# Order of steps at the passage into layer 1 and in its loop, and the place of the last row tile's listing, in a four-layer graph network

## The chip, the cores and the metric

One Trainium2 chip, one core, one launch. The metric is device microseconds (us) of the whole launch. TensorE (PE) multiplies matrices, VectorE (DVE), ScalarE (ACT) and GpSimd (POOL) work element by element, and SyncE (SP) issues most of the transfers (DMAs). Each engine works through its own queue in order, and semaphores make one engine wait for another.

## The reference

The input is a matrix `x` of 2708 nodes by 128 features and a symmetric-patterned adjacency `adj` of 2708 by 2708, about 0.6% of it non-zero. Four layers follow each other, each `x = x + layer(relu(layernorm(x)), adj)`:

```
layer 0:  msg = adj.T @ h;  msg / adj.sum(axis=0)[:, None]
layer 1:  s = h @ msg_w[:, :D].T ; d = h @ msg_w[:, D:].T
          messages[i, j] = gelu(s[i] + d[j] + msg_b)
          agg[i] = sum_j adj[i, j] * messages[i, j]
          layernorm(gelu([h, agg] @ upd_w.T + upd_b) + h) * ln_w + ln_b
layer 2:  a GRU cell on relu((adj @ h) @ W_msg.T + b_msg)
layer 3:  two attention heads, masked by adj > 0 and the diagonal
```

The change lies in the end of layer 0 and in layer 1.

## The kernel before

**Layer 0.** Nodes are cut into 22 tiles of 128 rows (the last has 20), and these into 6 groups of four. `order` runs over columns of groups `c` and, in each, row groups `s`; a "cut" (c, s) is one 512x512 piece of `adj`. `work_cut` (from line 366) transposes the cut on PE into `p_T` (L403), has ACT copy it out and sum it (`aT`, L410), multiplies it on PE (`sums`, L388), and, between these, takes one step at a time from a generator: `next_steps(c, s)` gives, by stage, the finishing work of the column before (`lift`, `spread`, `sum_rows` L260, `sum_squares` L270, `normal_rows` L137, `last_destinations`). `list_cut` has DVE list each cut's non-zeros: for each row of a 128x128 block the eight largest values (MAX8, L356) and their columns (FIND_INDEX8, L358). The last column (c = LAST = 5, tiles named `z`) is worked among the cuts of column 4, and `list_last` lists some of its rows.

**What layer 1 prepares for a row tile t.** `count_some` or `count_rows` counts the non-zeros of each row and block (`rows_n`), `rank` turns counts into first slots by a matmul (`p_r`, L551, copied to `ends`), `spread_ends` and `select_rows` make a step function over 128 slots per block (`sel`, L558 and L601), which SP shifts by one row through a DMA (`later`, L620 and L621), and `finish_rows` subtracts (`sel - later`, L625), which leaves a one-hot row for each slot. The values are split in three bf16 parts (the "rests"): lead (`lead_of`, ACT L568), rest (DVE L571, in the passage `less_lead` L586), its cast on ACT (L572, in the passage L590) and the last part on POOL (L573, L591, with L580 and L581 behind). `fetch` (PE L639, read out on ACT as `lead`, L640) brings the values into the slots, `place` (DVE L652 to L673) picks the one of each slot and its column (`where`), `pass_on` (PE `p_w` L689, ACT `where_T` L691, SP L693) and `spread_columns` (SP L699) send the columns through DRAM to all partitions, and `columns` (DVE L973) makes them one-hot (`cols`). `put_values` (POOL L956) and `put_more` (ACT L965) make the weights. `destinations`, `take_lead` and `split_rest` (PE L232, ACT L240, DVE L247, ACT L253, POOL L254) make `d`, also in three parts, for a group of tiles; `sources` and `sources_rest` (PE L710, DVE L728, ACT L568, DVE L571, ACT L572, POOL L573) make `s`.

**The loop.** `period(t)` has six steps k. In each, `combine` (PE `p_m`, L1012 with `sel` and L1016 with `cols`), `activate` (ACT `g`, L1024, with two `p_m` buffers) and `gather` (PE `agg`, L1037) work on tile t; around them stand the columns and weights of t+1, the fetch and place of t+2, rank, selection, rests and finish of t+3 and the count of t+4. `update(g, step)` finishes a group of four tiles over eight later periods; steps 2, 3, 5 and 6 (and 0) have DVE work. `sources` runs in even periods. `list_late` lists, on DVE, blocks that layer 0 left out (rows 17 to 20 and, by `LAST_AT`, the ends of rows 6 to 16) from tiles `cols_a` that SP loads a period ahead (`load_late`); two blocks at k = 1, the rest at k = 5. The last row tile of 20 rows is listed in one go with its blocks side by side on the partitions (`load_wide`, `list_wide`), and `place_wide` copies the result to its place with twelve small DMAs: in period `WIDE_AT` = 17. The order in every queue is the order of the code (`manual_schedule`).

Before period 0, `run(...)` and `opening` hold what has no earlier period to stand in. In the text below a number in brackets is a tile or a group: `finish_rows(2)`, `split_rest(4)`.

Of the kernel before, what the change touches and what calls it, by code (L numbers as in the profile page):

```python
# [20 lines left out]
F32 = mybir.dt.float32  # L21
# [9 lines left out]
P = 128  # L31
N = 2708
# [28 lines left out]
def listed_layers(ctx: ExitStack, tc: tile.TileContext, x, adj, w, out, flag):  # L61
# [454 lines left out]
    def next_steps(c, s):  # L516

        off = 1 if c < LAST - 1 else 0
        stage = s - 1 - off
        if stage == -1:  # L520
            return lift(c - 1)
        if stage == 0:
            return spread(c - 1)
        if stage == 1:
            return sum_rows(c - 1)
        if stage == 2:
            return sum_squares(c - 1)
        if stage == 3:
            return normal_rows(h, c - 1)
        return last_destinations() if stage == 4 and c == LAST - 1 else ()  # L530

    def last_destinations():
        destinations(LAST - 2)
        yield
        pass_on(0)
        project(0)
        turn_sums(LAST)
        yield

    def list_last(n):  # L540
# [41 lines left out]

    def less_lead(t):
        dst, src = values_of(t)
        rest = state["x", t] = opener.tile([P, NB, S], F32, name="hot")
        nc.vector.tensor_tensor(rest, src, dst[0], ALU.subtract)  # L586

    def pass_rest(t):
# [144 lines left out]
    for i, (c, s) in enumerate(order):  # L733
        g0, gk = GROUPS[s]
        list_cut(c, s, g0)
        if i == 0:
            state["f", 0] = factors(*state.pop(("m", -1)))
            list_cut(c, s, g0 + 1)
            state["m", 1] = moments(tiles_of(xs, *GROUPS[1]), "n4")
            list_cut(c, s, g0 + 2)  # L740
            state["f", 1] = factors(*state.pop(("m", 1)))
            list_cut(c, s, g0 + 3)
        else:
            for n in range(g0 + 1, g0 + gk):
                if c > 0 and s == (2 if c < LAST - 1 else 1) and n == g0 + 1:
                    invert(c - 1)
                list_cut(c, s, n)
            if c == LAST - 1:
                for n in {0: range(FIRST), 1: range(FIRST, 4), 2: range(4, HELD), LAST: range(NT - 2, NT)}.get(s, ()):
                    list_last(n)  # L750
                if s == 0:
                    count_some(0, FIRST)
                if s == 1:
                    count_some(FIRST, 1)
        if i + 1 < len(order):
            mask_near(*order[i + 1])
        if i > BEHIND and i - 1 - BEHIND + RING < len(order):
            load_cut(*order[i - 1 - BEHIND + RING])
        for z in {(LAST - 2, 3): (0,), (LAST - 2, 4): (1,), (LAST - 2, 5): (2,), (LAST - 1, 0): (3,), (LAST - 1, 2): (4,), (LAST - 1, 3): (5,)}.get(
            (c, s), ()  # L760
        ):
            load_cut(LAST, z)
        if (c, s) == (LAST - 1, 2):
            shift_rows(0)
        if c > 0 and s == (2 if c < LAST - 1 else 1):
            turn_sums(c - 1)
        if (c, s) == (LAST - 1, LAST):
            turn_rows(LAST - 2)
        work_cut(c, s, first_steps(s) if c == 0 else next_steps(c, s))
        if c > 1 and s == 3:  # L770
            split_rest(c - 2)
        if (c, s) == (LAST - 1, 3):
            pass_rest(0)
        if c > 1 and s == 0:
            turn_rows(c - 2)
        if c > 1 and s == 1:
            destinations(c - 2)
        if c > 1 and s == 2:
            take_lead(c - 2)
        if c == LAST - 1:  # L780
            if s == 1:
                ranked = rank(0, FIRST, bank("p_r"))
            for z in PARTS.get(s, ()):
                mask_near(LAST, z)
                work_cut(LAST, z)
            if s == 1:
                nc.vector.tensor_copy(*ranked)
                spread_ends(0)
                select_rows(0)
                lead_of(*values_of(0))  # L790
            if s == 2:
                less_lead(0)
                finish_rows(0)
            if s == 3:
                for q in range(2):
                    fetch(0, q)
            if s == LAST - 1:
                place(0)
                lead_of(*values_of(2))
                less_lead(2)  # L800
                for _ in lift(LAST):
                    pass

        if (c, s) == (1, 2):
            nc.sync.dma_start(msg_wT, w["msg_wT"])
        if (c, s) == (2, 3):
            nc.sync.dma_start(msg_b, w["msg_b"].partition_broadcast(P))
            nc.gpsimd.tensor_copy(src_self[:, 0, :], msg_wT[:, 0, :])
            nc.gpsimd.tensor_tensor(src_self[:, 1, :], msg_wT[:, 0, :], msg_wT[:, 1, :], ALU.add)

    write_one()

    pass_rest(2)
    lead_of(*values_of(1))
    take_lead(LAST - 2, pool.tile([P, 4, D], F32, bufs=1, name="part_x"))
    add(LAST)
# [12 lines left out]

# [31 lines left out]
    with (  # L861
# [9 lines left out]
        def count_rows(t):  # L871
            some = work.tile([P, NB, S], BF16, name="some")
            nc.vector.tensor_scalar(some, val[:, t, :, :], 0.0, None, ALU.is_gt)
            with nc.allow_low_precision("counts up to 8"):
                nc.vector.reduce_sum(rows_n[:, t, :], some, AX.X)

        def load_late(t):

            units = late_blocks[(t - 1) * AT_ONCE : t * AT_ONCE] if t > 0 else []
            if not units:  # L880
                return
            wide = N - LAST * CH
            flat_cols = work.tile([P, AT_ONCE * JB + wide], F32, name="cols_a")
            cols = flat_cols[:, 0 : AT_ONCE * JB].rearrange("p (b e) -> p b e", e=JB)
# [23 lines left out]
        def list_late(t, first, last):  # L908
# [6 lines left out]
        WIDE_AT = (len(late_blocks) + AT_ONCE - 1) // AT_ONCE + 1  # L915
        pieces = [(b, min(WIDE, NB - 1 - b)) for b in range(0, NB - 1, WIDE)]

        def load_wide():
            cols = work.tile([P, AT_ONCE * JB + N - LAST * CH], F32, name="cols_a")
            cols = state["wide"] = cols[:, 0 : AT_ONCE * JB].rearrange("p (b e) -> p b e", e=JB)  # L920
            for i, (b, k) in enumerate(pieces):
                nc.sync.dma_start(
                    cols[i * TAIL : (i + 1) * TAIL, 0:k, :],
                    adj[FULL * P : N, b * JB : (b + k) * JB].rearrange("r (b e) -> r b e", e=JB),
                )

        def list_wide():
            cols = state.pop("wide")
# [198 lines left out]
        def period(t, opening):  # L1127
# [6 lines left out]
            for k in range(GB):  # L1134
# [3 lines left out]
                if k == 0 and c and begun:  # L1138
                    pass_on(t + 1)
                    spread_columns(t + 1)  # L1140
                if k == 1 and a:
                    nc.vector.tensor_copy(*rank(t + 3, 1, rpool.tile([P, CH], F32, tag="r", name="p_r")))
                    spread_ends(t + 3)
                if k == 1 and last:
# [18 lines left out]
                    lead_of(*values_of(t + 3))  # L1163
                if k == 1:
                    list_late(t, 0, EARLY)
                    if t == WIDE_AT:
                        list_wide()
# [25 lines left out]
                if k == 4 and a and not begun:  # L1193
                    select_rows(t + 3)
                    describe_rest(t + 3)
                if k == (4 if begun else GB - 1) and a:
                    finish_rows(t + 3)
                if k in (0, 3):
                    load_next()
                if k == 4:  # L1200
                    load_late(t + 1)
                    if t + 1 == WIDE_AT:
                        load_wide()
                for g, step in updates.pop((t, k), ()):
                    update(g, step)
                if k == GB - 1:
                    list_late(t, EARLY, None)
                    if now and NT - 2 <= t + 4 < NT:
                        count_rows(t + 4)


# [11 lines left out]
        def take_pair(g):  # L1223
# [6 lines left out]
        )  # L1230
        opening = {
            1: ((turn_rows, 4), (fetch_both, 1), (select_rows, 2), (put_more, 0, 1)),
            2: ((destinations, 4), (put_more, 0, 2), (put_more, 0, 3), (place, 1), (take_lead, 4), (finish_rows, 2)),
            3: ((split_rest, 4), (pass_on, 1), (spread_columns, 1), (put_more, 0, 4), (put_more, 0, 5)),
            4: ((fetch_both, 2), (find_rows, 1), (put_values, 1)),
            5: ((place, 2),),
        }
# [880 lines left out]
```

## Time and profile before

| what | value |
|---|---|
| time of the launch, median of 3 | 987.94 us (986.31 to 989.44) |
| profiled execution: its time, its span | 986.58 us, 984.8 us |
| busy share PE, DVE, ACT, POOL | 93%, 81%, 54%, 45% |
| mean granted TensorE clock | 0.968 |
| the loop of layer 1, first L1016 to last L1045 | 205.8 to 543.5 us |

Times within the launch are microseconds from the start of the span. A row of the timeline gives start, duration, engine, line, operation, output and input, the count, and in brackets how long the engine had been idle and who ended that. A row of waits gives who waited for whom, the total, the number of times and the longest. In a table of windows each engine has its busy time, and behind the engines stand the granted clock (1.00 is full speed), the share of the DMA engines and GB/s. A line number can be that of a helper, so the tile's name tells which step it is.

### The profile page before, as it was taken

How to read it: one execution, taken by the hardware profiler on the slowest of the kernel's cores; microseconds unless marked ns; L12 is line 12 of the kernel's file. 1: busy time of each engine (PE TensorE's matmuls, PEld its weight loads, DVE VectorE, ACT ScalarE, POOL GpSimd, SP SyncE). 2: the span in 40 equal slices, each digit the busy share in tenths (PEclk: the TensorE clock that was granted, in tenths of full speed). 3: DMA queues.
4: the chain of work that ended last, by engine and by line, in shares of the span. 5: the costliest groups of instructions: out<-in, count | busy, mean ns of one | idle time of the engine just before them, and what ended most of it. 6: DMA issues, size and time to landing. Idle time of an engine off the chain costs nothing. (4 is left out here: it accounts for less than half of the span.)

```text
span 984.8 us, 21973 instructions
## 1 busy us (share of the span) xinstructions
PE 911.1 (93%) x7948; PEld 742.5 (75%) x7948; DVE 797.0 (81%) x2753; ACT 531.8 (54%) x1561; POOL 444.1 (45%) x524
## 2 busy tenths in 40 slices
PE   6799999768999999899999999999789999999983
PEld 3465556558999999898999444444678999999972
DVE  7999999788988989889674756566689877997793
ACT  5766776656666756676566123433222553655242
POOL 5402221369976787969765634444111300430132
PEclk9999999978999999999999899999899999999996
DMA  9899998325543434323215355564301674456000
GB/s 334 286 354 365 359 368 296 125 94 160 169 129 117 149 115 135 120 81 132 91 62 190 119 190 208 194 237 134 93 6 57 211 245 151 145 186 208 1 17 15
DMA packets 81736, 163.61 MB, mean 166 GB/s; under 512 B 9100, under 2 KB 27056, under 8 KB 81618
## 3 DMA queue, kind: packets, MB, share of 16 engines
q1 hardware_dynamic: 62518, 129.98, 40.8%
q10 hardware_dynamic: 19100, 32.13, 9.0%
q8 instruction: 64, 1.05, 0.5%
q14 instruction: 54, 0.44, 0.1%
HBM read 115.47 MB, written 30.87 MB: 149 GB/s over the span
## 5 line engine op out<-in xcount | busy, mean ns | idle before, releaser
L1327 PE MATMUL att<-hv,wt 128*128 128x129 f32 x1672 | 195.7, 278 | 7.9 <-DVE wt L1297 6.4
L956 POOL TENSOR_SCALAR put<-count,line,value 128x128 f32<-128x128 f32 x176 | 197.6, 1134 | 11.1 <-DVE value L673 10.4
L1327 PEld LDWEIGHTS att<-hv,wt 128*128 128x128 f32 x1672 | 191.9, 194 | 10.9 <-DVE wt L1297 8.9
L1016 PE MATMUL p_m<-d,cols 128*128 128x128 bf16 (+1 forms) x1452 | 162.6, 221 | 9.2 <-DVE cols L973 4.3
L1012 PE MATMUL p_m<-s,sel 128*128 128x128 bf16 x1452 | 162.4, 221 | 5.0 <-ACT g L1024 4.9
L1297 DVE SCALAR_TENSOR_TENSOR wt<-row,lift,mask 128x1024 f32<-128x1024 f32 (+1 forms) x132 | 138.8, 1083 | 22.2 <-PE att L1327 22.2
L121 POOL TENSOR_TENSOR n_r<-n_r,minus_half 128x4 f32<-128x4 f32 (+1 forms) x28 | 38.9, 1389 | 237.7 <-DVE n_r L120 236.0
L1037 PE MATMUL agg<-put,g 128*128 128x128 f32 (+1 forms) x968 | 126.8, 284 | 0.0
L1037 PEld LDWEIGHTS agg<-put,g 128*128 128x128 f32 x968 | 116.2, 196 | 2.4 <-issue 0.2
L388 PE MATMUL sums<-a,h 128*128 128x512 f32 x220 | 113.9, 613 | 1.6 <-ACT h L137 1.6
L1488 PE MATMUL p_agg<-a,hs 128*128 128x512 f32 (+2 forms) x264 | 108.8, 554 | 2.8 <-DMA a<-adjT 2.8
L1012 PEld LDWEIGHTS <-sel 128*128 128x128 bf16 x1452 | 103.9, 99 | 9.0 <-issue 8.3
L1016 PEld LDWEIGHTS <-cols 128*128 128x128 bf16 (+1 forms) x1452 | 101.9, 99 | 10.1 <-DVE cols L973 5.0
L1024 ACT ACTIVATE g<-p_m 128x512 f32<-128x512 f32 x132 | 72.7, 552 | 63.8 <-PE agg L1037 45.0
L403 PEld LDWEIGHTS p_T<-ident,a 128*128 128x128 f32 (+1 forms) x440 | 55.4, 144 | 60.7 <-issue 43.1
L965 ACT ACTIVATE put<-mine,value 128x128 f32<-128x128 bf16 x308 | 100.6, 392 | 0.0
L358 DVE FIND_INDEX8 col<-val,a 128x8 uint16<-128x128 f32 x327 | 91.6, 298 | 0.0
L410 ACT ACTIVATE aT<-p_T 128x512 f32<-128x512 f32 (+2 forms) x132 | 71.1, 541 | 27.5 <-PE p_T L403 26.6
L1488 PEld LDWEIGHTS p_agg<-a,hs 128*128 128x128 f32 (+1 forms) x264 | 47.5, 193 | 50.6 <-issue 46.3
L403 PE MATMUL p_T<-ident,a 128*128 128x128 f32 (+1 forms) x440 | 70.5, 281 | 11.9 <-DMA a<-in_adj 6.2
L1450 ACT ACTIVATE hs<-hs 128x1354 f32<-128x1354 f32 (+1 forms) x44 | 58.5, 1330 | 39.9 <-DMA hs<-in_adj 39.5
L356 DVE MAX8 val<-a 128x8 f32<-128x128 f32 x327 | 79.4, 289 | 0.0
(297 smaller groups left out, 1529.0 us busy)
## 6 DMA issues: line engine op xcount, KB each, us to landing
hs<-in_adj SPq DMA_DIRECT2D x42, 677.0 KB
adjT<-aT ACTq DMA_DIRECT2D x50, 512.0 KB
a<-adjT SPq DMA_DIRECT2D x20, 1280.0 KB
a<-in_adj SPq DMA_DIRECT2D x24, 1024.0 KB
spread<-passed SPq DMA_DIRECT2D x22, 704.0 KB
later<-sel SPq DMA_DIRECT2D x22, 616.0 KB
cols_a<-in_adj SPq DMA_DIRECT2D x11, 320.0 KB
row<-own_d ACTq DMA_DIRECT2D x10, 256.0 KB
```

Of the source, the lines that this page charges most:

```text
L356: nc.vector.max(val[0:m, n, b, :], v)
L358: nc.vector.max_index(col[0:m, n, b, :], val[0:m, n, b, :], v)
L388: nc.tensor.matmul(accs[c][:, 0:w], h0[0:m, n, :], a[0:m, n - g0, t0 * P - lo : t0 * P - lo + w], start=(n == 0), stop=(n == NT - 1),)
L403: nc.tensor.transpose(p[0:k, i * iw + q * P : i * iw + q * P + m], a[0:m, q, e : e + k], ident[0:m, 0:m])
L956: nc.gpsimd.tensor_scalar(st["put", 0][:, b, :], count, st["line"][:, b : b + 1], st["value"][:, b : b + 1], ALU.is_equal, ALU.mult,)
L965: nc.scalar.activation(st["put", 1][:, b - HP, :], st["mine"][:, b - HP, :], AF.Identity, scale=st["value"][:, b : b + 1])
L1012: nc.tensor.matmul(p[:, b - b0, :], st["sel"][:, b, :], s3[:, q, t % 2, :], start=(q == 0), stop=False)
L1016: nc.tensor.matmul(p[:, b - b0, :], st["cols"][0:kb, b, :], d3[0:kb, b, q, :], start=False, stop=(q == 2))
L1037: nc.tensor.matmul(agg, g[:, b - 4 * k, :], put, start=(b == 0), stop=False)
L1297: nc.vector.scalar_tensor_tensor(wt[:, 0:n], row[:, k, c : c + n], lift[:, j, k : k + 1], mask[:, j, c : c + n], op0=ALU.max, op1=ALU.mult,)
L1327: nc.tensor.matmul(banks[s // 3][:, s % 3, :], wt[:, q * P : (q + 1) * P], hv[:, j, k, :], start=(v < 2 and s // 3 not in touched), stop=( ...
L1488: nc.tensor.matmul(pa[:, 0:n], h[0:k, j, :], a[0:k, j - j0, 0:n], start=(j == 0), stop=(j == NT - 1))
```

## The change

It moves steps; the arithmetic stays. In the passage: one more tile's rows are listed and counted ahead of the ranking (tile 3, now ranked with the first three), and tile 4 is counted there too, so that period 0 of the loop has no rank and no count. `pass_rest(0)` stands ahead of the squares instead of behind `split_rest`; `project(0)` and the leads of tiles 2 and 1 move into the steps of cut (4, 4); `less_lead(1)` (into the buffer `picked`, since `hot` is taken), `spread_ends(1)` and `add_bias` move ahead of the last listing; `destinations(3)` and `pass_on(0)` stand ahead of cut (4, 5), `turn_rows(3)` ahead of them. In the opening, `split_rest(4)` comes one step earlier and `finish_rows(2)` one later. In every period, `describe_rest` and `sources_rest` stand ahead of `select_rows`, and `finish_rows` behind the updates. The last row tile is loaded and listed in period 12, its twelve copies are issued in period 13; periods 12 to 15 list 2, 6, 6 and 6 other blocks instead of 5 each. Tile 21 is counted in k = 2 of period 17.

```
 next_steps(c, s), c = LAST - 1:
+    stage 2: in_turn(in_order((pass_rest, 0)), squares)
+    stage 3: in_turn(in_order((project, 0), (lead_of, *values_of(2)), (lead_of, *values_of(1))), normal_rows(h, c - 1))
+    stage 4: in_order((pass_rest, 2), (pass_rest, 1), (turn_sums, LAST))
-    stage 4: last_destinations()   # destinations(3); yield; pass_on(0); project(0); turn_sums(5); yield
...
-                for n in {0: range(FIRST), 1: range(FIRST, 4), 2: range(4, HELD), LAST: range(NT - 2, NT)}.get(s, ()):
+                for n in {0: range(FIRST + 1), 2: range(4, HELD), LAST: range(NT - 2, NT)}.get(s, ()):
                     list_last(n)
                 if s == 0:
                     count_some(0, FIRST)
-                if s == 1:
                     count_some(FIRST, 1)
+                if s == 2:
+                    count_some(FIRST + 1, 1)
...
         if (c, s) == (LAST - 1, LAST):
-            turn_rows(LAST - 2)
+            destinations(LAST - 2)
+            pass_on(0)
         work_cut(c, s, first_steps(s) if c == 0 else next_steps(c, s))
...
-        if (c, s) == (LAST - 1, 3):
-            pass_rest(0)
...
-                ranked = rank(0, FIRST, bank("p_r"))
+                ranked = rank(0, FIRST + 1, bank("p_r"))
             for z in PARTS.get(s, ()):
                 mask_near(LAST, z)
                 work_cut(LAST, z)
+                if z == LAST - 1:
+                    turn_rows(LAST - 2)
...
                 place(0)
-                lead_of(*values_of(2))
                 less_lead(2)
+                less_lead(1)
+                spread_ends(1)
+                add_bias(0, d_rest.rearrange("p (t c) d -> p t c d", t=2))
...
-    pass_rest(2)
-    lead_of(*values_of(1))
     take_lead(LAST - 2, pool.tile([P, 4, D], F32, bufs=1, name="part_x"))
     add(LAST)
     measure(LAST)
-    less_lead(1)
-    add_bias(0, d_rest.rearrange("p (t c) d -> p t c d", t=2))
-    spread_ends(1)
...
-    pass_rest(1)
...
+        WIDE_AT = LATER - HELD + 1
+        for t in range(1, NT):
+            n = AT_ONCE + 1 - WIDE if t == WIDE_AT else AT_ONCE + (WIDE_AT < t < WIDE_AT + WIDE)
+            late_at[t], rest = rest[:n], rest[n:]
...
 period(t):
-                if k == 1 and a:
+                if k == 1 and a and not begun:
+                    spread_ends(t + 3)
+                elif k == 1 and a:
                     nc.vector.tensor_copy(*rank(t + 3, 1, ...))
                     spread_ends(t + 3)
...
                     if now and t % 2 == 0 and t + 2 < NT:
                         sources(t // 2 + 1)
                     if a and begun:
-                        select_rows(t + 3)
                         describe_rest(t + 3)
                     if now and t % 2 == 0 and t + 2 < NT:
                         sources_rest(t // 2 + 1)
-                    if now and t + 4 < NT - 2:
+                    if a and begun:
+                        select_rows(t + 3)
+                    if now and begun and t + 4 < NT and t + 4 != NT - 2:
                         count_rows(t + 4)
...
-                if k == 3 and t == WIDE_AT:
+                if k == 3 and t == WIDE_AT + 1:
                     place_wide()
...
-                if k == (4 if begun else GB - 1) and a:
+                if k == GB - 1 and a and not begun:
                     finish_rows(t + 3)
...
                 for g, step in updates.pop((t, k), ()):
                     update(g, step)
+                if k == 4 and a and begun:
+                    finish_rows(t + 3)
                 if k == GB - 1:
                     list_late(t, EARLY, None)
+                    if t == WIDE_AT:
+                        list_wide()
...
 opening (before period 0's steps k = 1, 2, 3):
             1: ((turn_rows, 4), (fetch_both, 1), (select_rows, 2), (put_more, 0, 1)),
-            2: ((destinations, 4), ..., (place, 1), (take_lead, 4), (finish_rows, 2)),
-            3: ((split_rest, 4), (pass_on, 1), (spread_columns, 1), ...),
+            2: ((destinations, 4), ..., (place, 1), (take_lead, 4), (split_rest, 4)),
+            3: ((finish_rows, 2), (pass_on, 1), (spread_columns, 1), ...),
```

More of the change, by code (lines that the diff above doesn't have):

```diff
@@ L526, in next_steps, with in_order @@
         if stage == 2:
-            return sum_squares(c - 1)
+            squares = sum_squares(c - 1)
+            return in_turn(in_order((pass_rest, 0)), squares) if c == LAST - 1 else squares
         if stage == 3:
[L529 to L537, printed above, removed]
+            last = c == LAST - 1
+            return in_turn(in_order((project, 0), (lead_of, *values_of(2)), (lead_of, *values_of(1))), normal_rows(h, c - 1)) if last else normal_rows(h, c - 1)
+        if stage == 4 and c == LAST - 1:
+            return in_order((pass_rest, 2), (pass_rest, 1), (turn_sums, LAST))
+        return ()
+    def in_order(*steps):
+        for step, *numbers in steps:
+            step(*numbers)
         yield
@@ L584, in less_lead @@
         dst, src = values_of(t)
-        rest = state["x", t] = opener.tile([P, NB, S], F32, name="hot")
+        if t == 1:
+            rest = opener.tile([P, NB, 4, S], F32, name="picked").rearrange("p b q s -> p (b q s)")[:, 0 : NB * S]
+            rest = rest.rearrange("p (b s) -> p b s", s=S)
+        else:
+            rest = opener.tile([P, NB, S], F32, name="hot")
+        state["x", t] = rest
         nc.vector.tensor_tensor(rest, src, dst[0], ALU.subtract)
@@ L875, in count_rows @@
                 nc.vector.reduce_sum(rows_n[:, t, :], some, AX.X)
+        WIDE_AT = LATER - HELD + 1
+        pieces = [(b, min(WIDE, NB - 1 - b)) for b in range(0, NB - 1, WIDE)]
+        late_at, rest = {}, list(late_blocks)
+        for t in range(1, NT):
+            n = AT_ONCE + 1 - WIDE if t == WIDE_AT else AT_ONCE + (WIDE_AT < t < WIDE_AT + WIDE)
+            late_at[t], rest = rest[:n], rest[n:]
         def load_late(t):
-            units = late_blocks[(t - 1) * AT_ONCE : t * AT_ONCE] if t > 0 else []
+            units = late_at.get(t, [])
             if not units:
@@ L882, in load_late @@
             wide = N - LAST * CH
+            base = WIDE if t == WIDE_AT else 0
             flat_cols = work.tile([P, AT_ONCE * JB + wide], F32, name="cols_a")
-            cols = flat_cols[:, 0 : AT_ONCE * JB].rearrange("p (b e) -> p b e", e=JB)
+            whole = flat_cols[:, 0 : (AT_ONCE + 1) * JB].rearrange("p (b e) -> p b e", e=JB)
+            cols = whole[:, base:, :]
+            if base:
+                state["wide"] = whole
+                for i, (b, k) in enumerate(pieces):
+                    nc.sync.dma_start(
+                        whole[i * TAIL : (i + 1) * TAIL, 0:k, :],
+                        adj[FULL * P : N, b * JB : (b + k) * JB].rearrange("r (b e) -> r b e", e=JB),
+                    )
             state["late", t] = []
@@ L913, in list_late @@
                 nc.vector.max_index(col[0 : size(n), n, b, :], val[0 : size(n), n, b, :], a)
[L915 to L925, printed above, removed]
         def list_wide():
@@ L1165, in period @@
                     list_late(t, 0, EARLY)
-                    if t == WIDE_AT:
-                        list_wide()
                 if k == 2:
@@ L1201, in period @@
                     load_late(t + 1)
-                    if t + 1 == WIDE_AT:
-                        load_wide()
                 for g, step in updates.pop((t, k), ()):
                     update(g, step)
+                if k == 4 and a and begun:
+                    finish_rows(t + 3)
                 if k == GB - 1:
                     list_late(t, EARLY, None)
-                    if now and NT - 2 <= t + 4 < NT:
+                    if t == WIDE_AT:
+                        list_wide()
+                    if now and t + 4 == NT - 2:
                         count_rows(t + 4)
@@ L1232, in listed_layers @@
             1: ((turn_rows, 4), (fetch_both, 1), (select_rows, 2), (put_more, 0, 1)),
-            2: ((destinations, 4), (put_more, 0, 2), (put_more, 0, 3), (place, 1), (take_lead, 4), (finish_rows, 2)),
-            3: ((split_rest, 4), (pass_on, 1), (spread_columns, 1), (put_more, 0, 4), (put_more, 0, 5)),
+            2: ((destinations, 4), (put_more, 0, 2), (put_more, 0, 3), (place, 1), (take_lead, 4), (split_rest, 4)),
+            3: ((finish_rows, 2), (pass_on, 1), (spread_columns, 1), (put_more, 0, 4), (put_more, 0, 5)),
             4: ((fetch_both, 2), (find_rows, 1), (put_values, 1)),
```

## The prediction

> **What bounds the kernel now.** First the page's slices, to see where PE is not full.
>
> ```profile
> PE   6799999768999999899999999999789999999983
> PEclk9999999978999999999999899999899999999996
> ```
>
> Slices 7 and 8 (172 to 221 us) are the passage; the loop behind it is full but for small dents. Then the waits of 130 to 200 and PE's own of 195 to 560, which name the dents.
>
> ```profile
> PE y L639 <- POOL xb L581: 4.8, 1, 4.8
> ACT part_x L467 <- DVE inv_deg L441: 2.3, 1, 2.3
> PE p_r L551 <- ACT part_x L467: 0.4, 1, 0.4
> ```
> ```profile
> PE p_m L1012 <- ACT g L1024: 4.9, 4, 2.5
> PE p_m L1016 <- DVE cols L973: 4.3, 2, 3.5
> PE p_m L1016 <- ACT d L253: 2.6, 1, 2.6
> PE p_m L1016 <- POOL d L254: 2.4, 1, 2.4
> PE p_r L551 <- DVE rows_n L875: 0.8, 1, 0.8
> ```
>
> By the timeline these end at 178.6 (4.76), 205.8 (3.51), 221.9 (2.60) and 224.4 (2.35) in the passage; in the loop at 402.2 (2.49, period 12), 463.5 (1.64, period 16) and 487.0 (0.85, period 18). Windows of 1 and 2 us give their aftermath:
>
> ```profile
> 400.00:402.00 2.00, 0.00 (x0) 0.00 (x0) 1.86 (x5) 1.97 (x7) 2.00 (x3) 1.00 1.03 318
> 404.00:405.00 1.00, 1.00 (x6) 1.00 (x6) 1.00 (x2) 1.00 (x4) 1.00 (x2) 0.50 0.00 0
> 465.00:466.00 1.00, 1.00 (x7) 1.00 (x6) 1.00 (x2) 1.00 (x5) 1.00 (x1) 0.50 0.11 37
> 486.00:488.00 2.00, 1.15 (x13) 1.02 (x10) 1.44 (x5) 0.00 (x0) 2.00 (x3) 1.00 0.06 11
> ```
>
> The stalls of 2.49 and 1.64 are followed by some 3.3 us at clock 0.50, so each costs 1.65 more; that of 0.85 is not. From one `p_w` to the next, an even period without a stall takes 14.45 us, period 12 takes 18.73, 16 takes 17.88, 18 takes 15.68: 4.28 + 3.43 + 1.23 = 8.94 us are lost there.
>
> By the Trainium skill ("TensorE: Matmul & The Clock Gate", Part 1) the clock halves after an idle window of about 3.4 us. By that rule alone 1.64 us of idleness would cost no clock; the row at 465 says 0.50, and the rows decide. By the rule the two loop stalls would be worth 3.3 us less.
>
> All positions are those of the profile of before; "comes to" is the same axis with what stands ahead moved.
>
> **The passage up to `cols(0)`.** Listing tile 3 early puts its two `z` blocks (157.78 to 158.46, 0.69) and its count (0.53) ahead of `inv_deg`: 1.22 us on DVE, which `part_x` already waits for, and `p_r` for that. So PE comes to the fetch at about 175.2 instead of 173.8. That cost is hidden under the 4.76; without this cover it would be 1.2, or 2.9 with the clock. `pass_rest(0)` now runs ahead of the squares: rest on DVE at 171.1 (170.50 + 0.53 for counting tile 4, 0.1 to pass on), ACT L590 0.3, POOL L591 to L581 1.2: 172.7, where it had ended at 178.5. `sel` is finished at 172.03 + 0.53 = 172.6. The fetch runs when PE arrives, 175.2 instead of 178.6.
>
> What then sets the end is DVE. It worked without a gap from 169.65 to 185.50; with 0.53 of counting, two rests (0.26 each), `ends4` (0.11), `add_bias` (0.60) and the last listing (190.40 to 191.43, 1.03) it comes to 188.3. `p_d(3)` is there: 175.2 + 0.7 fetch + 8.0 for cut (4, 4) and its `z` piece with `project` + 0.5 + 1.6 + 1.0 = 187.0, and ACT's copy 0.6. So `take_lead(3)` starts at about 188.4 instead of 192.60, 4.2 us earlier. From there to `cols(0)` at 204.77 all is DVE's chain. The rest, bias and `ends4` that leave it (0.97) stood in the time in which DVE would have waited for POOL's power (195.60 to 196.57), so leaving saves nothing; 12.17 us remain. `turn_sums(4)` needs 192 to 193, its reader 197.3; the spread is issued 5 us earlier. Gain 4.1, between 2.5 (a listing that waits for its load, the clock) and 4.2.
>
> **The opening.** `split_rest(4)` leaves its place behind the sources: ACT L253 follows the six puts (end 215.48), POOL L254 the eight puts (end 216.35). With 1.15 (176.39) to 2.49 (221.88) for it, `d` is complete by 217.5 to 218.8, not 224.4; PE wants it at 219.6. The price: `finish_rows(2)` now waits for `s`. ACT: 215.48 + 0.52 + 0.5 (`g`) + 0.3 = 216.9, `s_r` to 217.2, L625 1.62: 218.85, so the fetch starts 0.5 later. 2.60 and 2.35 vanish, and PE would start period 1 at about 223.9 instead of 230.5. What is late next is `cols(1)`: ACT's `where_T` comes to 218.8 (was 221.71, behind the sources), spread issued at 220.4 (223.30) and landed 4.4 us later as before (227.68 - 223.30): 224.8, plus 0.95. So L1016 of period 1 starts at 225.8 instead of 230.7: 4.9. PE has then stood idle 1.9, and 3.3 us at half clock follow, behind 230.5 in the old run they are over: 4.9 - 1.65 = 3.3. I take 3.3, as 1.64 was enough for the clock; range 2 to 4.9.
>
> Edits with one answer: the wider rank (88 instead of 66 columns) and the missing count, rank and copy of period 0 (0.24 + 0.34 + 0.17 on DVE) lie ahead of waits that stay; the earlier leads of tiles 2 and 1 and `turn_rows(3)` use up ACT's waits of 3.63 at 179 and are in PE's 187.0; the early `pass_on(0)` only moves its DMA away from the last `adjT` stores. If POOL's or ACT's cover were gone, each would cost its own length, 0.3 to 0.8.
>
> **The loop.** Rests ahead of the selection: where DVE is late, as in period 12, ACT gets `s_r` 1.5 us sooner. Where DVE is early it is the reverse. Period 10:
>
> ```profile
> 365.34 0.69 DVE L728 TENSOR_TENSOR sb<-p_s,msg_b 128x512 f32<-128x512 f32 x1 [1.13 <-PE p_s L710]
> 365.95 1.61 DVE L601 TENSOR_TENSOR sel<-count_h,ends 128x2816 bf16<-128x2816 bf16 x1
> 367.48 0.34 DVE L571 TENSOR_TENSOR v_r<-val,xb 128x176 f32<-128x176 f32 x1
> 368.04 0.42 DVE L571 TENSOR_TENSOR s_r<-sb,s 128x256 f32<-128x256 f32 x1 [0.23 <-ACT s L568]
> ```
>
> `s_r` needs ACT's lead of `s`, which follows PE's second fetch at 367.2 and ends at 368.0 in either order. The selection filled that time; now DVE stands, and selection, `cols`, `place` and the listing behind them come 1.5 us later. The periods with `mix` (5, 9, 13) do likewise: `xb` is ready at 413.7 and DVE free at 410.9. Slack absorbs that up to period 9; from 368 to 396 DVE has no wait left.
>
> `finish_rows` behind the updates: it comes later by their DVE time, 2.5 us for step 2 or 5, 1.15 for 3 or 6. In period 10: 373.85 + 1.5 + 2.5 + 1.62 = 379.5, the fetch stands at 378.71: stall 0.8. Period 11: 388.02 + 1.5 + 3.65 + 1.62 = 394.8 against 393.16 + 0.8: 0.8. Period 12: `sb` ends at 398.7, `s_r` 399.5, then as before 2.3 us on ACT to `g`, which ends at 402.4, PE arrives at 401.3: 1.1. Sum 2.7 instead of 2.49, but in pieces of about 1, which may spare the clock: -1.6 to +0.2, I take -0.8.
>
> The twelve copies move to period 13. They hold SP:
>
> ```profile
> 476.33 1.01 SPq L942 DMA_DIRECT2D val<-tops  x1
> ...
> 485.00 0.72 SPq L942 DMA_DIRECT2D col<-tops_at  x1
> ```
>
> That is 9.4 us, in 17 with no load behind them. In 13 they start behind `later` at 417.6 and end at 427.0; `load_late(14)` and `passed(15)` (423.85 before) are queued behind. Six blocks land at about 430 (transfer estimated from `later`, landed 3.3 us after its last issue), DVE wants the first two at 425.3 and stands. `sb` comes to 431.4 instead of 428.0: `g` of period 14 1.5 us too late, then fetches in 15 and 16 by 0.7 and 0.9, since listing six also adds 0.46 in each of 13 to 15, and `g` in 16 by 0.9. Sum 3.8, with one or two halvings 5.5 to 7; before, 3.43. I take +1.7, range 0 to +3.8. The six wide loads (3.0 us of SP) now stand ahead of `passed(13)`, but end at 389.8, when it is due: nothing; the wide listing (1.84 on DVE) takes the place of other blocks in 12 and leaves 17, which had slack. Period 18's 1.23 goes: tile 21 is counted early and no longer waits 3.07 for its copies. Loop: -0.8 + 1.7 - 1.2 = -0.3, from -2.8 to +2.8.
>
> **Sum.** 986.58 - 4.1 - 3.3 - 0.3 = 978.9 for the profiled execution. The median of before lies 1.36 above its profiled run: 980.2.
>
> **The rivals.** (a) The loop gains all it lost: DVE slack takes the waits, neither stall nor half clock remains. 987.94 - 7.4 - 8.9 = 971.6. For it: in the even periods 2 to 6 and 14 DVE waits over 1 us for PE today; against: DVE without a gap in 10 to 12.
> (b) Slower: DVE becomes the bound of the loop. From 262 to 408 it is busy 132.6 of 146 us, 13 us per period of 14.2. If 1.5 us of standing comes in each of periods 8 to 16, it exceeds PE by some 0.3 to 1.2 each, and every second overrun halves the clock: 9 x 0.8 + 5 x 1.65 + the copies' 4 = 19, against which stand 3.43 + 4.28 + 7.4 = 15.1 saved: 987.94 + 3.9 = 992. It decides from the point where DVE's wait for `p_r` vanishes in all of 8 to 16; that two even periods have over 2 us of slack speaks against.
> (c) The passage does not pass its gain on: the listings of cut (4, 4) wait for loads, or a POOL step at 2.49 instead of 1.15 holds period 0; half of 7.4 lost: 984 to 986.
>
> **How the numbers follow.** Forecast 0.60, (a) 0.14, (b) 0.12, (c) 0.14. The measurement can tell about 0.3%, 3 us. The forecast's own range is 975 to 985; to hold 8 in 10 it reaches into (a) and (c): 973 to 987. Faster: 0.57 + 0.14 + 0.04 = 0.75; same 0.13; slower 0.12.
>
> **What would show it.** Right: the fetch `y` without a wait for POOL at 175; `cols(0)` near 200.6; no wait for L253 or L254; PE's next wait at `cols(1)`; 7 us less between the first cut of column 4 and the second `p_w`. In the loop a wait of `v_r` or `s_r` on ACT in front of `sel`, waits of L639 for L625 in 11 and 15, a DVE wait for `cols_a` in 14, none at `rows_n`. Wrong: `cols(0)` at 204, or PE idle in most periods.

## The result, and the profile after

984.82 us (median of 7, 982.60 to 985.46) against 987.94 us before (7 runs, 986.31 to 990.04): 0.9965 of before, 95% interval 0.9950 to 0.9979. The forecast was a gain of 7.7 us; 3.1 came. The profiled execution of after took 985.46 us with a span of 983.7 us. It was the slowest of the seven, so positions inside the launch are compared and not the two spans.

The measure is `p_w`, which PE runs once per tile: `p_w(i)`, i counted from 0, opens period i - 1. In the table, "lead" is its position after minus before, and a period lasts from one `p_w` to the next.

| stretch | before, us | after, us | lead at its end, us |
|---|---|---|---|
| up to period 1 (`p_w(2)`) | 231.87 | 224.84 | -7.03 |
| period 1 | 13.57 | 15.55 | -5.05 |
| periods 2 to 10 | 130.21 | 130.10 | -5.16 |
| period 11 | 13.57 | 14.35 | -4.38 |
| period 12 | 18.73 | 16.52 | -6.59 |
| period 13 | 15.37 | 15.36 | -6.60 |
| period 14 | 14.44 | 19.98 | -1.06 |
| period 15 | 13.58 | 13.58 | -1.06 |
| period 16 | 17.88 | 14.53 | -4.41 |
| period 17 | 15.36 | 17.80 | -1.97 |
| period 18 | 15.68 | 14.65 | -3.00 |
| period 19 | 13.52 | 13.67 | -2.85 |

So passage and opening give 7.0 (7.4 were forecast); period 1 takes 2.0 back, and the loop behind it 2.2 more. Each column is one profiled execution: five kernels below with the same code up to `p_w(2)` (passage_only, copies_spread, wide_late, order_back, copies_early) have -6.77 to -8.40 there. What lies behind the loop scatters: from `p_w(21)` to the end of the span the profiled runs below took between 468.5 us (order_back) and 472.9 us (rest_first), on the same code.

The page's slices, counted from 0 as in the prediction: PE is fuller in slices 7 and 8 (9 and 8 tenths instead of 7 and 6) and in 16 (no dent any more), and the clock has a new dent in slice 17, 418 to 443 us. Then PE's waits of 195 to 560, and the waits of 130 to 200.

```profile
PE   6799999988999999999999999999789999999982
PEclk9999999879999999989999899999899999999996
```
```profile
PE p_m L1025 <- DVE cols L982: 4.9, 3, 2.9
PE p_m L1021 <- ACT g L1033: 4.4, 5, 2.3
PE y L646 <- DVE sel L632: 2.8, 3, 1.4
PE p_r L553 <- DVE rows_n L880: 2.3, 1, 2.3
PE y L646 <- POOL xb L583: 1.8, 1, 1.8
```
```profile
ACT part_x L467 <- DVE inv_deg L441: 3.7, 1, 3.7
PE p_r L553 <- ACT part_x L467: 2.0, 1, 2.0
```

The waits for `d` (2.60 and 2.35) are gone, and so is the 4.76 of the fetch on POOL: its 1.8 here is another fetch's. Of the three waits for `sel`, two are new; the one at 216.8 in the opening was 0.54 before and is 1.43 now. The timeline of after gives the waits their places; the brackets hold the idle time and who ended it.

```profile
184.93 0.66 PE L150 MATMUL p_h<-ident,hs 128*128 128x128 f32 x4 [1.39 <-DVE picked L670]
203.17 0.50 PE L1025 MATMUL p_m<-d,cols 128*128 128x128 bf16 x3 [2.86 <-DVE cols L982]
216.82 0.72 PE L646 MATMUL y<-xb,sel 128*128 128x37 bf16 x22 [1.43 <-DVE sel L632]
223.66 0.34 PE L1025 MATMUL p_m<-d,cols 128*128 128x128 bf16 x3 [1.43 <-DVE cols L982]
229.88 0.43 PE L646 MATMUL y<-xb,sel 128*128 128x37 bf16 x11 [1.81 <-POOL xb L583]
374.32 0.45 PE L646 MATMUL y<-xb,sel 128*128 128x37 bf16 x11 [0.61 <-DVE sel L632]
389.66 0.44 PE L646 MATMUL y<-xb,sel 128*128 128x37 bf16 x11 [0.72 <-DVE sel L632]
397.27 0.33 PE L1021 MATMUL p_m<-s,sel 128*128 128x128 bf16 x3 [1.02 <-ACT g L1033]
429.57 0.48 PE L1021 MATMUL p_m<-s,sel 128*128 128x128 bf16 x3 [2.34 <-ACT g L1033]
468.63 0.18 PE L553 MATMUL p_r<-rows_n,before 128*128 128x22 bf16 x1 [2.26 <-DVE rows_n L880]
```

The 2.34 in period 14 is what the twelve copies lead to. DVE waits for its late blocks, whose load SP issues only behind the copies:

```profile
424.19 0.49 DVE L932 MAX8 val<-cols_a 128x8 f32<-128x128 f32 x2 [4.92 <-DMA cols_a<-in_adj]
```
```profile
410.74 1.00 SPq L951 DMA_DIRECT2D val<-tops  x1
...
420.17 0.72 SPq L951 DMA_DIRECT2D col<-tops_at  x1
420.93 0.48 SPq L918 DMA_DIRECT2D cols_a<-in_adj  x1
```

The windows of after behind it show 6 us at half clock: period 14 is 5.54 longer, 2.34 in the wait and the other 3.2 there. Behind the 2.26 at 468 the clock stays full.

```profile
430.00:432.00 2.00, 2.00 (x14) 1.61 (x12) 1.83 (x6) 2.00 (x7) 0.00 (x0) 0.50 0.99 299
434.00:436.00 2.00, 2.00 (x17) 1.94 (x17) 1.86 (x8) 0.42 (x2) 0.00 (x0) 0.50 0.00 2
470.00:472.00 2.00, 2.00 (x21) 2.00 (x20) 0.00 (x0) 0.50 (x1) 2.00 (x3) 1.00 0.08 34
```

And the wait in period 1: the last parts of `xb(3)`, which the fetch of tile 3 reads, stand on POOL behind the eight puts of tile 1. First before, then after:

```profile
224.36 8.84 POOL L956 TENSOR_SCALAR put<-count,line,value 128x128 f32<-128x128 f32 x8
```
```profile
217.28 11.54 POOL L965 TENSOR_SCALAR put<-count,line,value 128x128 f32<-128x128 f32 x8
...
229.56 0.27 POOL L583 COPY xb<-ends 128x22 bf16<-128x22 bf16 x1
```

PE comes to this fetch at 228.07 instead of 234.94, 6.9 us earlier, and POOL begins its puts 7.1 us earlier. But the same eight puts take 2.70 us longer: three of them last 3.25, 2.34 and 2.12 us, the other five 0.79 each. So `xb(3)` ends at 229.83 instead of 234.21, only 4.4 us earlier. With the 8.84 us of before it would have ended at about 227.1, ahead of PE.

### The profile page after: what moved, and what is told of

Its sections match the earlier page's. It is cut to its first block, busy times and chain, and to the rows that moved or that the text cites. A ratio compares the mean times of both kernels' runs of the same rounds, so it can differ in the third digit from the quotient of the medians.

```text
span 983.7 us, 21963 instructions
## 1 busy us (share of the span) xinstructions
PE 912.6 (93%) x7947; PEld 742.6 (75%) x7947; DVE 796.4 (81%) x2752; ACT 531.1 (54%) x1561; POOL 453.9 (46%) x524
## 3 DMA queue, kind: packets, MB, share of 16 engines
q8 instruction: 64, 1.05, 0.5%
## 5 line engine op out<-in xcount | busy, mean ns | idle before, releaser
L965 POOL TENSOR_SCALAR put<-count,line,value 128x128 f32<-128x128 f32 x176 | 195.5, 1122 | 13.2 <-DVE value L680 13.2
L121 POOL TENSOR_TENSOR n_r<-n_r,minus_half 128x4 f32<-128x4 f32 (+1 forms) x28 | 42.8, 1529 | 237.3 <-DVE n_r L120 235.6
L358 DVE FIND_INDEX8 col<-val,a 128x8 uint16<-128x128 f32 x327 | 89.6, 286 | 0.0
L356 DVE MAX8 val<-a 128x8 f32<-128x128 f32 x327 | 77.4, 277 | 0.0
```

The costliest lines, as they stand in the source:

```text
L356: nc.vector.max(val[0:m, n, b, :], v)
L358: nc.vector.max_index(col[0:m, n, b, :], val[0:m, n, b, :], v)
L965: nc.gpsimd.tensor_scalar(st["put", 0][:, b, :], count, st["line"][:, b : b + 1], st["value"][:, b : b + 1], ALU.is_equal, ALU.mult,)
```

## The experiments

Each kernel was profiled and timed beside before on the same chip, where the median of before was 986.5 to 987.3 us. Ratios are to that before, with 95% intervals; many of them overlap, so two variants often can't be told apart by their times. Leads are as above, in us; "loop" is the lead at `p_w(21)` minus that at `p_w(3)`, what the loop from period 2 on adds. All leads come from one profiled execution each, and where the clock halves changes from one to the next: behind the same code period 1 lasts 15.54 us in copies_early and 17.15 in wide_late.

| kernel | `p_w(2)` | `p_w(3)` | `p_w(15)` | `p_w(21)` | loop | median us | ratio |
|---|---|---|---|---|---|---|---|
| after | -7.03 | -5.05 | -6.60 | -2.85 | +2.20 | 984.82 | 0.9965 (0.9950 to 0.9979) |
| passage_only | -8.40 | -2.51 | -2.75 | -3.80 | -1.29 | 981.79 | 0.9945 (0.9924 to 0.9966) |
| loop_only | +0.57 | +0.57 | -1.07 | +2.36 | +1.79 | 989.87 | 1.0021 (1.0006 to 1.0036) |
| copies_spread | -6.77 | -3.23 | -4.86 | -4.43 | -1.20 | 980.39 | 0.9935 (0.9911 to 0.9959) |
| wide_late | -8.31 | -4.73 | -6.37 | +1.69 | +6.42 | 986.39 | 0.9991 (0.9975 to 1.0007) |
| rest_first | -8.31 | -8.30 | -9.94 | -5.03 | +3.27 | 982.58 | 0.9959 (0.9942 to 0.9976) |
| order_back | -8.40 | -2.52 | -2.77 | -4.25 | -1.73 | 983.46 | 0.9962 (0.9944 to 0.9981) |
| other_bank | -7.89 | -5.94 | -7.51 | -2.42 | +3.52 | 983.57 | 0.9963 (0.9948 to 0.9978) |
| all_three | -8.22 | -8.22 | -9.86 | -7.82 | +0.40 | 979.12 | 0.9931 (0.9907 to 0.9955) |
| copies_early | -8.36 | -6.39 | -7.95 | -3.21 | +3.18 | 983.45 | 0.9967 (0.9945 to 0.9988) |
| three_finish | -7.92 | -7.91 | -6.76 | -4.47 | +3.44 | 980.35 | 0.9937 (0.9914 to 0.9960) |
| three_old | -8.55 | -8.54 | -8.72 | -9.04 | -0.50 | 977.78 | 0.9916 (0.9883 to 0.9949) |
| three_mixed | -8.80 | -8.79 | -10.44 | -10.60 | -1.81 | 976.15 | 0.9889 (0.9859 to 0.9920) |

**passage_only**

```
 # the loop of before:
+ if a and begun: select_rows(t + 3); describe_rest(t + 3)   # and then sources_rest
+ if k == (4 if begun else GB - 1) and a: finish_rows(t + 3)
+ wide list in period 17, late blocks five at a time
```

> The new passage and opening with the loop of before (selection ahead of the rests, end of the selection ahead of the updates, wide list in period 17). Theory A (the passage gives 5, the loop takes 2 back): p_w of tile 2 stands 5.0 us earlier than before, as in the profile after, every later period keeps that to within 0.5, and the kernel takes 983.0 (982 to 984), 5 under before. Theory B (the loop's edits are neutral, the passage passes on less than the trace shows, since the list of later tiles and the stages behind the loop wait for something else): the lead shrinks along the loop and the kernel takes 984.8 like after.

Neither theory held as written. The lead at `p_w(2)` is 8.4, more than in after, but period 1 lasts 19.46 and takes 5.9 of it: the same wait for `xb(3)`, here 3.09 us, followed by clock 0.50 up to about 235. The eight puts take 11.55 us here too, and the first step of `xb(3)` behind them 1.80 us instead of 0.53, beside the selection that DVE does at that moment in the old order.

```profile
229.79 0.51 PE L646 MATMUL y<-xb,sel 128*128 128x37 bf16 x11 [3.09 <-POOL xb L583]
```

From there the lead grows a little instead of shrinking. So the loop of before keeps what it is given, and period 1 is a loss of its own.

**loop_only**

```
-            2: (..., (take_lead, 4), (split_rest, 4)),      # opening and passage of before
+            2: (..., (take_lead, 4), (finish_rows, 2)),
```

> The passage and opening of before with the new loop (rests ahead of the selection, its end behind the updates, wide list in period 12 and its twelve copies in period 13). Theory A: periods 2 to 11 last 13.57 as before, the lead is 0 up to there, and between periods 11 and 19 about 2.2 us are lost net, period 14 lasting 5.5 more than before: 990.2 (989 to 991.5). Theory B: 988 (within 0.8 of before).

Theory A: the loss of 1.8 is there without the new passage, in period 14 (+1.85), 15 (+1.62) and 17 (+2.42), against gains in 12, 16 and 18. Period 14 does not lose the 5.5 that the theory named: its wait for `g` is 1.70 us and no half clock follows, and the wait of 1.44 for `sel` in period 15 comes in its place. The wait for `rows_n` in period 17 is 2.25 us, though PE comes to that period 0.8 us later than before.

**copies_spread**

```
-                if k == 3 and t == WIDE_AT + 1: place_wide()
...
                     load_late(t + 1)
+                    if 1 <= t - WIDE_AT <= 3: place_wide(2 * (t - WIDE_AT - 1))   # four copies
```

> The kernel after with the twelve copies of the wide list in three lots of four, in periods 13, 14 and 15, each behind that period's load on SP instead of all twelve ahead of it. Theory A (the copies hold up the load of cols_a for period 14, DVE waits 4.92 us for it, PE 2.34 us, and then the clock stands at 0.50 for two windows): DVE's wait at 424 us goes, PE's 2.34 us stall at 429 goes, period 14 lasts about 14.5 instead of 19.98; period 16, which lasted 3.4 less than before, gives some of that back: 981.5 (980 to 983). Theory C (DVE itself is late in period 14 because it does more than before, and the load only ends last): the wait moves to another releaser, period 14 stays over 18 us, and the kernel takes 984.8 like after.

Theory A: DVE's wait for `cols_a` and the 2.34 are gone, period 14 lasts 14.44. Period 16 gives 1.8 of the 5.5 back (16.30 against 14.53). The loop now gains 1.2.

**wide_late**

```
-        WIDE_AT = LATER - HELD + 1
+        WIDE_AT = (len(late_blocks) + AT_ONCE - 1) // AT_ONCE + 1    # 17; loads and copies as before
```

> The kernel after with the wide list back in period 17, its loads and copies with it, and with the loads of the late blocks as before; the new order of rests, selection and updates stays. Theory A: period 14 lasts 14.4 as before, period 17's stall of 1.23 is back, and what is left of the loop's loss is the new order's alone (fetch stalls of 0.6 and 0.7, wait for g of 1.0 in periods 10 to 12): 982.5 (981.5 to 984). Theory C: the new order itself costs the loop its 2.2 us, and the kernel takes 984.8 like after.

Both theories were wrong: period 14 is back at 14.44, yet the loop loses 6.4, nearly all in periods 17 and 18 (19.75 and 20.09, before 15.36 and 15.68). DVE has the wide list there on top of what the new order put later, and PE waits 2.59 and 3.74 us for `rows_n`. The edit also puts the count of tile 21 back to the end of period 17, as before (so does passage_only), which adds to the wait in 18. The new order with the list and this count as before is worse than with both early.

**rest_first**

```
-            4: ((fetch_both, 2), (find_rows, 1), (put_values, 1)),
+            4: ((fetch_both, 2), (find_rows, 1), (put_values, 1, 0, 3)),    # three of eight puts
...
                     describe_rest(t + 3)
+                    put_values(t + 1, 3)                                     # the other five
```

> The kernel after, but in the opening only three of the eight puts of tile 1 stand on POOL ahead of the three steps that finish xb of tile 3; the other five come behind them. Theory A (fetch of tile 3 waits 1.81 us for xb, since POOL does the eight puts first, 11.54 us): the wait goes, period 1 lasts 13.6 to 14.0 instead of 15.55 and nothing in period 2 gives it back: 1.5 to 2.5 us under after, that is 982.7 beside a before of 987.9. Theory D (POOL is the bound of the opening: it is busy in every window from 216 to 240): the wait moves to agg, which reads the puts, and period 1 stays above 15 us: no gain.

Theory A: the wait is gone, period 1 lasts 13.58, and the lead of 8.3 is whole at `p_w(3)`, 3.25 more than in after. At the loop's end 2.2 of it are left: period 17 lasts 19.33, with the wait of 2.25 for `rows_n` that after has too. The trace shows the gain, the time does not: 0.9959 of before against 0.9965.

**order_back**

```
                     if a and begun:
+                        select_rows(t + 3)
                         describe_rest(t + 3)
...
-                if k == 4 and a and begun: finish_rows(t + 3)     # behind the updates
+                if k == (4 if begun else GB - 1) and a: finish_rows(t + 3)   # ahead of them
```

> The kernel after with the old order in the loop (selection ahead of the rests, end of the selection ahead of the updates), the wide list still in period 12. With passage_only, wide_late and after it makes the four cases of two edits. Theory E (DVE is packed from period 10 on; the new order puts the selection's end behind updates and so costs stalls of 0.6 and 0.7 in periods 11 and 12, but saves 2.1 in period 12 where g waits less; the twelve copies cost their 5.5 whatever the order): period 11 back at 13.57, period 12 near 18.6, period 14 near 20: 986. Theory F (order and wide list add up, with no cross term: passage_only stands at 0.9945 of before, wide_late at 0.9991, after at 0.9965): 0.992 of before, 980.

Theory E was right on periods 11 and 12 (13.57 and 18.61), and wrong on the copies: period 14 lasts 14.44. F's 0.992 did not come either: the two edits do not simply add up. The four cases by their loop column: old order and list in 17 -1.3, old and 12 -1.7, new and 17 +6.4, new and 12 +2.2. By these profiles the new order costs 4 us with the early list and 8 with the late one; the early list is worth 0.4 in the old order. The times agree on the late list (0.9991 against 0.9945), but they do not tell order_back from after (0.9962 and 0.9965), and the profiled execution of order_back was its fastest. Why the copies cost nothing in the old order, its queue shows:

```profile
409.68 0.56 SPq L627 DMA_DIRECT2D later<-sel  x1
...
411.18 0.98 SPq L951 DMA_DIRECT2D val<-tops  x1
...
420.66 0.48 SPq L918 DMA_DIRECT2D cols_a<-in_adj  x1
```
```profile
424.02 0.49 DVE L932 MAX8 val<-cols_a 128x8 f32<-128x128 f32 x2 [1.37 <-DMA cols_a<-in_adj]
```

The shifts `later` wait for the selection, and the copies stand behind them. Here period 13 begins at 405.19, so the copies start 6.0 us into it; in after it begins at 401.36 and they start at 9.4. The 3.4 us that the selection moved are carried by SP's queue over the copies to the load.

**other_bank**

```
-                    turn_rows(LAST - 2)
+                    turn_rows(LAST - 2, turnp.tile([P, CH], F32, name="p_T"))
```

> The kernel after, with the turned rows of group 3 in a PSUM tile of the transposes' pool instead of the bank that follows y0 of tile 0. Theory A (PE waits 1.39 us at 184.9 for the bank that place(0) still reads, and the clock that falls to 0.50 for it until 196 makes the passage 1 us later): the wait goes, p_w of tile 0 stands near 188.0 instead of 188.9 and cols(0) near 201.9 instead of 202.2 to 203: 0.5 to 1.3 under after. Theory G (DVE sets the pace of the passage, PE is only ahead of it by that wait, and waits later instead): within 0.5 of after.

The wait of 1.39 is gone and the clock stays full at 188. `p_w(0)` stands at 188.48 and not at 188.9, the lead at `p_w(2)` is 0.9 better, and the time does not tell it from after. But this profile can't settle the theories: its clock was 0.50 from about 158 to 161, so PE comes to the fetch at 176.47 instead of 174.84. passage_only came as late (176.45) and has no such wait with the old bank either. all_three, below, has the new bank and a fetch at 174.79: `p_w(0)` stands at 186.80, against 188.05 and 188.03 in wide_late and rest_first, which have the wait (1.40 and 1.46) with the clock full. PE's first `cols` there is 0.7 us earlier, and at `p_w(2)` the lead is 8.22 against 8.31. So the wait costs 1.2 us at `p_w(0)` and nothing clear at `p_w(2)`: theory G is the better one.

**all_three**

```
 copies_spread + rest_first + other_bank
```

> The kernel after with the twelve copies in three lots behind the loads, with xb of tile 3 ahead of five of the puts of tile 1, and with the other PSUM tile. If the three act on different stages (Theory A throughout) the gains add: copies 3 to 5, xb 2, bank 0 to 1.3, that is 976 to 979 beside a before of 987.3. If the later stages only keep what one of them gives, 980.4 like copies_spread.

Up to period 16 the trace keeps the gains of the puts and of the spread copies (lead 9.5 at `p_w(17)`); period 17 then lasts 19.43. 979.1 is the upper end of what was expected.

**copies_early**

```
                 if k == 2:
+                    if t == WIDE_AT + 1: place_wide()      # ahead of the selection and its shifts
```

> The kernel after with all twelve copies together in period 13, but at the head of the period's third step, ahead of the selection's two shifts on SP instead of behind them. Theory H (the load of cols_a is late because the copies wait behind the shifts, and the new order has put the selection and so the shifts 3.4 us later in the period: the copies start 9.4 us after p_w in after, 6.0 in order_back): copies from 404, shifts near 413, load of cols_a near 415 instead of 420.9, DVE's wait for it under 1 us and period 14 back at 14.4 to 15: 3 to 5 under after, 0.992 to 0.9935 of before. Theory I (twelve copies in a row cost the same wherever they stand, since now the shifts are late): the end of the selection waits for the shifts, fetch of tile 16 stalls by 2 to 4, no gain over after.

H was right on the queue (copies from 403.42, load at 415.16) and wrong on the gain. Theory I is nearer: DVE now waits 4.29 us for the shifts instead of 4.92 for the load, though the stalls of PE are smaller than I said (0.54 at the fetch, then 0.79 and 1.24).

```profile
413.23 0.56 SPq L627 DMA_DIRECT2D later<-sel  x1
...
415.16 0.57 SPq L918 DMA_DIRECT2D cols_a<-in_adj  x1
```
```profile
418.13 1.82 DVE L632 TENSOR_TENSOR sel<-sel,later 128x2816 bf16<-128x2816 bf16 x1 [4.29 <-DMA later<-sel]
```

Periods 14 and 15 lose 3.1 together. It is the block of twelve that costs, not its place alone.

**three_finish**

```
 all_three, and finish_rows(t + 3) ahead of the updates; the rests stay ahead of the selection
```

> The kernel all_three with the end of the selection ahead of the updates again; the rests stay ahead of the selection. If the updates ahead of the end of the selection cause the fetch stalls (0.51, 0.72, 0.23, 0.54 us on sel) and the packed DVE of period 16, these go: periods 11 and 12 lose 1.2 less, 1 to 3 under all_three, 976.5. If the late selection itself causes them, nothing changes: 979.1.

The waits for `sel` are gone, but those for `g` are larger: 2.54 in period 12 instead of 1.02, 3.65 in period 16 instead of 0.99, and a new one of 1.05 in period 8. So the end of the selection behind the updates is what spares `g`, and the fetch stalls of 0.5 to 0.7 are its price. The time is 980.35 (0.9937), not the 976.5 that was expected.

**three_old**

```
 all_three with the old order in every period
```

> The kernel all_three with the old order in the loop. By the lengths of the periods in order_back (period 12 18.61 against 16.52, period 16 16.92 against 16.31, period 17 15.86 against 19.43): 1.5 to 2 under all_three, 977.5; if period 12 takes more because it comes earlier, 979.

As expected: period 12 lasts 18.67, period 17 15.37. 977.8 lies within the runs' scatter of all_three (975.98 to 983.61 against 977.92 to 981.90).

**three_mixed**

```
 all_three, with the new order for t <= 13 and the old one for t > 13
```

> The kernel all_three with the new order in periods 1 to 13 and the old order from period 14 on. By the lengths of the periods: 16.52 in period 12 as in after, 15.9 in period 17 as in order_back instead of 19.43: 2.5 to 3.5 under all_three, 976. If period 17's loss comes from the earlier arrival of PE and not from the order, 979 like all_three.

The lowest median of all: 976.15 us, 1.1% under before, and all of its 6 runs (975.53 to 976.53) are below the fastest of all_three. Against three_old, 1.6 us above it, the intervals overlap. Period 12 lasts 16.51 as in the new order, period 17 15.36 as in the old one; period 16 keeps one wait for `g` (2.51, 18.75 us).

## Why the prediction was right or wrong

**The passage up to `cols(0)`** (forecast -4.1). The fetch stands at 174.84, as forecast (175.2), without a wait for POOL. `take_lead(3)` came at 189.74 and not at 188.4, and PE's `cols` at 203.17 instead of 205.76 before: 2.6. The missed term is half clock behind the wait of 1.39 at 184.93, which makes `p_d(3)` late. It was not in the sum, and it is chance: where the same wait stands and the clock held (rest_first, wide_late), `take_lead(3)` comes at 188.8 to 188.9 and PE has `cols` at 201.9, a gain of 3.8.

**The opening** (forecast -3.3). Both waits for `d` vanished and `cols(1)` became the next one, as told. It came 1.43 after PE and no half clock followed, so the opening gave 4.4. The fetch behind `finish_rows(2)` paid 0.9 instead of 0.5. Together with the passage: 7.0 measured, 7.4 forecast, since the two misses offset each other, both by the clock.

**Period 1** (forecast 0). This is the first failed step. "What is late next" was followed to `cols(1)` and no further. The next user was the fetch of tile 3, whose `xb` parts stand behind eight puts on POOL, a term that the sum put at nothing. POOL came to these puts 7.1 us earlier, as PE came to the fetch 6.9 earlier, but at their new place they took 11.54 us instead of 8.84, and that makes the wait of 1.81. The slow ones run beside DVE's instructions on `mine`, `sel` and `cols`; that these slow them is a guess that no run tests. rest_first shows that the place behind the puts matters: with `xb(3)` ahead of five of them period 1 lasts 13.58. So the price was 2.0 in after, and 3.5 to 5.9 in copies_spread, wide_late and passage_only, where the clock fell too.

**The loop, periods 2 to 16** (forecast -0.8 for the order, +1.7 for the copies). The mechanisms came as written: `s_r` waits 1.45 us in front of `sel` in period 10 (forecast 1.5); the fetch waits 0.61 and 0.72 (0.8 each) and `g` 1.02 (1.1), without half clock; DVE stands for `cols_a` in period 14. Periods 11 and 12 give -1.4. The stall for `g` in 14 was 2.34 (1.5 forecast) and cost 5.5 with its half clock; the waits in 15 and 16 that were to follow did not, since DVE had caught up by then, and 16 lost 3.35 less. In loop_only, where the clock held behind the stall of 14, they did follow (1.44, 0.54 and 0.97). The four stalls of the forecast add up to 4.0 and not to the 3.8 it wrote, well inside its range. Sum over 14 to 16: +2.2 against +1.7, and +1.8 to +1.9 in loop_only, rest_first and other_bank.

**Period 17** (forecast: no wait at `rows_n`). The second failed step, +2.44. DVE counts tile 20 at the end of period 16, and PE's rank of it stands early in period 17. Before, PE lost 1.64 and half clock in period 16, and the count ended 0.3 us behind `p_w(18)` at 469.22. In after period 16 takes 14.53, and the count ends 3.8 us behind `p_w(18)` at 464.81. The count of before, of after and of loop_only:

```profile
469.15 0.34 DVE L875 TENSOR_REDUCE rows_n<-some 128x22 bf16<-128x176 bf16 x1
```
```profile
468.24 0.34 DVE L880 TENSOR_REDUCE rows_n<-some 128x22 bf16<-128x176 bf16 x1
```
```profile
473.44 0.34 DVE L875 TENSOR_REDUCE rows_n<-some 128x22 bf16<-128x176 bf16 x1
```

The forecast had counted only the gain of period 18 (-1.2; -1.03 measured) and given the stall of 16 no successor. The lead from the passage is not the reason: in loop_only `p_w(18)` stands at 470.03, 0.8 us later than before, and the count still ends 3.7 us behind it. In every kernel with the new order throughout that distance is 3.7 to 4.1 us, whatever its lead. It is 0.3 in three_old and 0.2 in three_mixed, which are 8.0 and 9.6 us ahead of before at `p_w(18)` and have no such wait; both have the old order from period 14 on, and there PE waits for `g` in period 16 instead (2.48 and 2.51). What decides is the order of the loop. Periods 16 and 17 together last 34.1 in three_mixed and 35.7 in all_three.

So of the 4.85 us between -7.7 and the -2.85 at the loop's end, 4.4 are the lengthening of the two periods whose waits were not looked for: one behind work that ran slower at its new place, one that an earlier stall had covered. Rival (b), DVE as the bound, is out: periods 8 to 16 lengthened by 0.7 us together, where it had 19 us of loss against some 8 of stalls saved. Rival (a), a loop without stalls, is out with a loop that lost 2.2. Rival (c) has the measured time in its range, 984 to 986, but partly by luck: its slow POOL step of period 0 did not come (1.16 us); POOL's slower puts, which hold period 1, are its nearest relative, and the rest was lost in the loop.

## What to carry to other kernels

When a stall ahead of PE is taken away, walk every later operand of PE up to the next place where PE already waited. Ask of each which queue makes it, what stands in front of it there, and whether that still takes as long at its new place: in period 1 eight puts took 2.7 us more. Ask of a stall that goes what it had covered: the one in period 16 had hidden a late count. A block of small copies on a queue should be cut up and put behind the load that is due next; moved as a block it only chooses who waits. And one order need not serve a whole loop: by the traces, the order that saved 1.5 us in periods 11 and 12 cost 2.2 in 14 to 17 (all_three against three_old), and taking each where it is better gave the lowest median, 1.6 us under the better of the two, which is about their scatter.

## What the hardware showed beyond that

The same idle time of PE halved the clock or did not. 1.39 us at 184.93 in after, the only wait of PE above 0.1 us from 157 to 190, was followed by clock 0.50 from about 187 on; 1.46 at 184.96 in rest_first was not, and its clock fell only at about 195. The wait of 1.64 for `g` in period 16 of before was followed by half clock, that of 1.65 in passage_only was not. The wait of 2.26 for `rows_n` cost period 17 2.4 us in after and 4.1 in all_three. First after, then rest_first, in the same window:

```profile
188.00:192.00 4.00, 4.00 (x18) 2.69 (x16) 2.44 (x12) 1.91 (x9) 0.71 (x2) 0.50 0.04 8
```
```profile
188.00:192.00 4.00, 3.94 (x17) 1.86 (x15) 3.29 (x15) 3.16 (x13) 1.96 (x6) 1.00 0.22 45
```

The forecast had treated the half clock as a threshold on the stall's length, between 0.85 and 1.64 us. By these rows it is a chance that goes with the stall. The Trainium skill ("TensorE: Matmul & The Clock Gate", Part 1) says of the first matmuls of a kernel that the activity window is free-running, so that the moment of the change depends on where in it they fall. Taken over to stalls, that would fit these pairs, though no run here shows the window itself. The length that the page gives for an idle window, about 3.4 us, does not fit: 1.39 us was enough here.
